# Query copies moved around VectorE's exps in a graph-attention kernel, and the last layers' loads put in program order on one queue

## The chip, the cores and the metric

The kernel runs on one core of one Trainium2 chip. The metric is the device time of one execution in microseconds. The kernel before the change takes 11197.88 us (median of three runs, 11197.59 to 11198.84).

## What is computed

Four graph layers run over the same 3327 x 128 features `x` and the same 3327 x 3327 float32 adjacency `adj`. Each layer adds its result to its input and normalises the rows.

```python
# layer 0: attention; d is the feature (128 of them act as heads), h has 8 values
q = (x @ Wq.T).reshape(d, n, h)          # likewise k and v
a = einsum('dnh,dmh->dnm', q, k) * scale + adj + adj
x = layernorm(x + einsum('dnm,dmh->dnh', softmax(a, axis=2), v).reshape(n, h*d) @ Wo.T)
# layer 1: x = layernorm(x + dinv * (adj + I) * dinv @ (x @ W.T + b)),  dinv = (row sums of adj + I)**-0.5
# layer 2: x = layernorm(x + (adj / row sums) @ x @ W_in + (adj.T / column sums) @ x @ W_out)
# layer 3: x = layernorm(x + x @ W_self.T + (adj @ x) @ W_neigh.T + b)
```

In layer 0 there are 128 score matrices of 3327 x 3327 whose exps have to be formed; that is most of the work.

## The kernel before

**Preparation** (the first 430 us of the trace) forms the projections of q, k and v in DRAM (`q_s`, `k_s`, `v_img`) and starts to write a tiled transpose of the adjacency (`adjT_s`).

**Attention** (`attention()`, about 430 to 10410 us) goes through 28 blocks. A block combines 476 query columns (`CW`) with one of four sets of key tiles, `KBS`, with 7, 7, 6 and 6 tiles of 128 keys: "7-tile" and "6-tile" blocks below. In a block, the 128 features are taken in 32 groups of 4 (`GROUP`). Group number `n` counts on over the blocks (0 to 895); even and odd groups are treated differently.

For each of the 4 features d of a group, three sets of key tiles follow one another (`SETS`: 3 + 2 + 2 tiles, or 2 + 2 + 2). One such set is called a place here; a group has 12. At each place:

- TensorE forms the scores into one of three PSUM tiles `sc` (L572; `kt` and `qt` are its operands). `sc` keeps the adjacency and adds only the difference between this feature and the one before it, which is why `qt` needs negated copies of the features' neighbours.
- ScalarE takes the exp of the tile into `e` (L580). In even groups the third set of the first feature is taken by VectorE instead: `vector_exp` reads the scores once (L536) and then works out the exp with eight more steps (L537, L538, L539, five times L542). In this document these eight are "the chain".
- TensorE weighs the values with the exps of the *group before* into the PSUM tile `o` (L597, `weigh`); at which places it does so is fixed in `PLACES`. The e tiles of VectorE belong to the third set, so that their weighs come late in the odd group that follows.

After every third group `flush` adds `o` to an accumulator on VectorE (L610, or L608 in the first set of keys).

**VectorE's order.** The orders of TensorE, ScalarE, VectorE and GpSimd in this part are those of the program. VectorE's smaller steps wait in a Python list `vec` and are handed out by `vector_work` at each place, as many as a count of estimated times (`clock`) allows; `weigh` forces out what a weigh needs. An entry of `vec` holds its cost, the group it belongs to (`of`; None for copies) and the step.

`copy_queries` gives the three steps that complete the next group's `qt` after its load: L465 and L466 write the negated neighbours into rows 32 to 63, L467 copies rows 0 to 63 into rows 64 to 127. Before, they are put at the *front* of `vec` at the second feature of each group:

```python
elif d % GROUP == 1 and n + 1 < len(groups):
    vec[0:0] = copy_queries(*groups[n + 1])
```

`load_heads` loads `qt` and `kt` two groups ahead from SyncE's queue (L435, L442). Every eighth group VectorE also works on a piece of the adjacency's transpose (`background_work`, L200 to L215).

**The last layers** (about 10410 us to the end) finish layer 0 and do layers 1 to 3. In the first stage, 26 row tiles are loaded from `o_s` (L1051, `divide`), divided (DVE L1053, GpSimd L1055), transposed (L1063), multiplied by `woT` (L1072, `outputs`), added to a tile of `x` (L88) and normalised. Then `gather` runs 26 times for layer 1, and again for layers 2 and 3: each loads 1.7 MB of `adjT_s` (tile `eT`, L1032) and does 26 matmuls (L1038). Layer 2 has also a pass over rows of `adj` (tile `a2`, L1141). `eT` and `a2` share five buffers (`big`). Before, even row tiles are loaded from SyncE's queue and odd ones from ScalarE's; only TensorE's order is fixed (`tc.manual_schedule`), and a scheduler chooses the order of the other engines, SyncE's loads among them.

Of the kernel before, what the change touches and what calls it, by code (L numbers as in the profile page):

```python
# [19 lines left out]
P = 128  # L20
GROUP = 4
# [29 lines left out]
def kernel(ctx: ExitStack, tc: tile.TileContext, x, adj, wq, wk, wv, wo,  # L51
# [14 lines left out]
    nc = tc.nc  # L66
    N, D = x.shape
# [18 lines left out]
    def load_rows(eng, sb, dram, t):  # L86
        for a, n in spans(tokens(t)):
            eng.dma_start(out=sb[a:a + n, :], in_=dram[t * P + a:t * P + a + n, :])  # L88

    def store_rows(eng, dram, sb, t):  # L90
        for a, n in spans(tokens(t)):
            eng.dma_start(out=dram[t * P + a:t * P + a + n, :], in_=sb[a:a + n, :])
# [29 lines left out]
    adjT_s = scratch.tile([T * P, T * P], F32, name="adjT_s")  # L122
# [258 lines left out]
    def attention():  # L381
        with tc.tile_pool(name="acc", bufs=1) as accp, tc.tile_pool(name="kq", bufs=3) as kq, \
# [129 lines left out]
            def prepare(b, d):  # L512

                n = b * NHG + d // GROUP
                if d % GROUP == 0:
                    if n + 2 < len(groups):
                        heads[groups[n + 2]] = load_heads(*groups[n + 2])
                    if n + 1 < len(groups):
                        values[groups[n + 1]] = load_values(*groups[n + 1])
                    while stores:  # L520
                        store(*stores.pop(0))
                    background(n)
                elif d % GROUP == 1 and n + 1 < len(groups):
                    vec[0:0] = copy_queries(*groups[n + 1])
                elif d % GROUP == 3:
                    background_work(n)

            vec = []
# [423 lines left out]

    w1T, w2, w3T, woT = (act.tile([P, w], F32, name=f"tw{i}") for i, w in enumerate((D, 2 * D, 2 * D, HD)))
    for sb, dram in ((w1T, w1T_s), (w3T, w3T_s), (woT, woT_s)):
        nc.sync.dma_start(out=sb, in_=dram)  # L955
    nc.sync.dma_start(out=w2[:, 0:D], in_=w2_in)
    nc.sync.dma_start(out=w2[:, D:2 * D], in_=w2_out)
    b1_sb = act.tile([1, D], F32, name="b1_sb")
    nc.sync.dma_start(out=b1_sb, in_=b1.unsqueeze(0))
    b3_sb = act.tile([1, D], F32, name="b3_sb")  # L960
    nc.sync.dma_start(out=b3_sb, in_=b3.unsqueeze(0))


    for i in range(4):
# [61 lines left out]
    def gather(t, y, col, b, meanwhile=()):  # L1026


        n = tokens(t)
        todo = list(meanwhile)  # L1030
        e = big.tile([P, T, P], F32, tag="big", name="eT")
        (nc.sync, nc.scalar)[t % 2].dma_start(out=e.rearrange("p s n -> p (s n)"), in_=adjT_s[t * P:(t + 1) * P, :])  # L1032
        ps = bank(b)
        for s in range(T):
            while todo and todo[0][0] <= s:
                todo.pop(0)[1]()
            m = tokens(s)
            nc.tensor.matmul(ps[:n, 0:D], lhsT=e[:m, s, :n], rhs=y[:m, s, col:col + D],  # L1038
                             start=(s == 0), stop=(s == T - 1))
        for _, what in todo:  # L1040
            what()
        return ps
# [48 lines left out]
        nc.vector.tensor_tensor(xs[1][:n, t, :], ps[:n, 0:D], xs[0][:n, t, :], ALU.add)  # L1091
        nc.scalar.copy(y3[:n, t, :], ps[:n, D:2 * D])

    with tc.manual_schedule(engines={mybir.EngineType.PE}):
        def stage0(t):
            if t < T:
                heads_turned(t)
            if 1 <= t <= T:
                outputs(t - 1)
            if 3 <= t <= T + 2:  # L1100
                turn(xs[0], t - 3, 4)
            if 4 <= t <= T + 3:
                support(t - 4)

        for t in range(T):
            divide(t)
            stage0(t)


        def after(src, t, finish):  # L1110
            return [(12, lambda: turn(src, t, 4)), (19, lambda: finish(t))] if t >= 0 else []

        for t in range(T):
            n = tokens(t)
            ps = gather(t, y1, 0, 6 + t % 2,
                        after(xs[1], t - 1, messages) if t else
                        [(2 + 5 * k, lambda k=k: stage0(T + k)) for k in range(4)])
            z = work.tile([P, D], F32, name="z")
            nc.vector.tensor_tensor(z[:n, :], ps[:n, 0:D], y1[:n, t, :], ALU.add)
            h = work.tile([P, D], F32, name="h")  # L1120
            nc.vector.scalar_tensor_tensor(h[:n, :], z[:n, :], dinv[:n, t:t + 1], xs[0][:n, t, :],
                                           ALU.mult, ALU.add)
            norm(n, h[:n, :], xs[1][:n, t, :])


        backT = act.tile([P, NP], F32, name="backT")
        cols = [(c, min(512, N - c)) for c in range(0, N, 512)]
        order = [6, 0, 1, 2, 3, 4, 5]
        acc = {}
        for t in range(T):  # L1130
            n = tokens(t)
            a = big.tile([P, T * P], F32, tag="big", name="a2")
            load_rows((nc.sync, nc.scalar)[t % 2], a[:, 0:N], adj, t)
            for i, (c, w) in enumerate(cols):
                if t == 0 and i == 3:
                    turn(xs[1], T - 1, 4)
                if t == 0 and i == 5:
                    messages(T - 1)
                if t == 0:
                    acc[i] = bank(order[i])  # L1140
                nc.tensor.matmul(acc[i][:, 0:w], lhsT=y2[:n, t, D:2 * D], rhs=a[:n, c:c + w],  # L1141
                                 start=(t == 0), stop=(t == T - 1))
        for i, (c, w) in enumerate(cols):
            copy(i, backT[:, c:c + w], acc[i][:, 0:w])


        for t in range(T):
            n = tokens(t)
            zs = {}

            def back(t=t, n=n):
                pb = bank(t % 2)
                nc.tensor.transpose(pb[:n, 0:P], backT[:, t * P:t * P + n], ident)  # L1153
                zs[t] = work.tile([P, D], F32, name="z")
                nc.vector.scalar_tensor_tensor(zs[t][:n, :], pb[:n, 0:D], inv_col[:n, t:t + 1], xs[1][:n, t, :],
                                               ALU.mult, ALU.add)

            ps = gather(t, y2, 0, 7 - t % 2, [(6, back)] + after(xs[0], t - 1, last_inputs))
            h = work.tile([P, D], F32, name="h")
            nc.vector.scalar_tensor_tensor(h[:n, :], ps[:n, 0:D], inv_row[:n, t:t + 1], zs[t][:n, :],  # L1160
                                           ALU.mult, ALU.add)
            norm(n, h[:n, :], xs[0][:n, t, :])


        for t in range(T):
            n = tokens(t)
            ps = gather(t, y3, 0, 6 + t % 2, after(xs[0], T - 1, last_inputs) if t == 0 else ())
            h = work.tile([P, D], F32, name="h")
            nc.vector.tensor_tensor(h[:n, :], ps[:n, 0:D], xs[1][:n, t, :], ALU.add)
            res = work.tile([P, D], F32, name="res")  # L1170
            norm(n, h[:n, :], res[:n, :])
            store_rows(nc.sync, out, res, t)


# [27 lines left out]
```

## Time and profile before

| what | value |
|---|---|
| median of three runs | 11197.88 us |
| profiled execution, its own time | 11193.06 us |
| its span, first to last instruction | 11191.2 us |
| mean granted TensorE clock | 0.988 |
| busy: TensorE, ScalarE, VectorE, GpSimd | 94%, 88%, 65%, 13% of the span |
| attention, first exp to last | 431 to 10407 us |
| a 7-tile block, a 6-tile block | about 372 us, about 340 us |
| last layers | 10410 to 11191 us |

A profile line begins with the source line and the engine: PE is TensorE's matmuls, PEld its weight loads, DVE VectorE, ACT ScalarE, POOL GpSimd, SP SyncE; a q behind an engine's name marks its sequencer, which also issues DMAs. Then come the operation, the tile written and the tiles read, the shape and the count. In the groups of the page, the numbers behind the bar are busy time in us and the mean of one in ns; behind the second bar stand the engine's idle time just before these instructions and what ended most of it. In a list of waits, a line gives the waiting engine and line, what it waited for, and then total us, times and the longest. In a timeline, a line gives the start and length in us; the idle time before it stands in brackets. Windows give busy time and instruction counts of each engine in a stretch, and at the end the granted clock, the DMA engines' share and GB/s. TensorE's ends are modelled, so that its busy time overstates how full it is.

### The profile page before, as it was taken

What the parts mean: (1) busy time and instruction counts of PE and PEld (TensorE: products, weight loads), DVE (VectorE), ACT (ScalarE), POOL (GpSimd) and SP (SyncE); (2) the same over time, 40 slices, a digit from 0 to 9 for tenths busy, and PEclk for the clock granted to TensorE, in tenths of its full rate; (3) what the DMA queues carried; (4) which work ended last, traced back from release to release, by engine and by line L of the source; (5) the groups of instructions that cost most, each with busy time, mean ns of one, the idle gap of its engine ahead of it and who ended that gap; (6) DMA issues with size and microseconds to landing.
All of it is one profiled execution on the core that took longest, in us unless ns stands there. A gap on an engine that the chain in (4) does not pass through costs nothing. (4 is left out here: it accounts for less than half of the span.)

```text
span 11191.2 us, 200920 instructions
## 1 busy us (share of the span) xinstructions
PE 10524.8 (94%) x76607; PEld 4034.8 (36%) x76607; DVE 7265.7 (65%) x8368; ACT 9856.7 (88%) x10746; POOL 1497.4 (13%) x2738
## 2 busy tenths in 40 slices
PE   6699999999999999999999999999999999999899
PEld 2233333333333333333333333333333333333779
DVE  6466777667776677766777666776666666666412
ACT  2599999999999999999999999999999999999400
POOL 4311122111121111211112100010000100000200
PEclk8799999999999999999999999999999999999999
DMA  8888888888888888888888888778887788877686
GB/s 288 197 126 123 124 128 133 123 127 125 127 132 123 127 126 128 130 126 127 124 128 130 122 121 120 119 118 119 116 114 114 115 118 116 115 109 113 192 284 245
DMA packets 989911, 1536.50 MB, mean 137 GB/s; under 512 B 202879, under 2 KB 799921, under 8 KB 974617
## 3 DMA queue, kind: packets, MB, share of 16 engines
q1 hardware_dynamic: 894410, 1292.54, 74.4%
q0 software_dynamic: 82432, 128.80, 4.5%
q10 hardware_dynamic: 12110, 102.22, 2.6%
q8 instruction: 621, 10.17, 0.5%
q14 instruction: 338, 2.77, 0.1%
HBM read 1378.68 MB, written 143.98 MB: 136 GB/s over the span
## 5 line engine op out<-in xcount | busy, mean ns | idle before, releaser
L580 ACT ACTIVATE e<-sc 128x952 f32<-128x952 f32 (+1 forms) x10304 | 9667.4, 1062 | 332.8 <-PE sc L572 294.8
L597 PE MATMUL o<-e,v_pad 128*32 128x476 f32 (+1 forms) x46592 | 5633.3, 573 | 227.6 <-DVE e L542 176.7
L572 PE MATMUL sc<-qt,kt 64*128 64x476 f32 x23296 | 4473.0, 438 | 187.2 <-ACT e L580 136.0
L572 PEld LDWEIGHTS sc<-qt,kt 64*128 64x128 f32 x23296 | 2170.2, 184 | 4510.2 <-ACT e L580 4229.0
L536 DVE TENSOR_SCALAR ey<-sc 128x952 f32<-128x952 f32 x448 | 515.1, 1150 | 2543.1 <-PE sc L572 2543.1
L597 PEld LDWEIGHTS o<-e,v_pad 128*32 128x32 f32 (+1 forms) x46592 | 1037.0, 108 | 2144.4 <-issue 1848.2
L542 DVE SCALAR_TENSOR_TENSOR e<-e,ey 128x952 f32<-128x952 f32 x1344 | 1545.0, 1150 | 38.6
L481 POOL COPY v_pad<-vs 128x192 f32<-128x192 f32 (+1 forms) x896 | 337.5, 403 | 8543.4 <-DMA vs<-v_img 5980.0
L467 DVE CAST qt<-qt 64x1904 fp32r<-64x1904 f32 x896 | 1035.6, 1156 | 30.5
L224 POOL DMA_DIRECT2D adjT_s<-at x1352 | 800.0, 599 | 223.3 <-DMA adjT_s<-at 82.7
L465 DVE TENSOR_SCALAR qt<-qt 32x1428 fp32r<-32x1428 f32 x896 | 803.8, 897 | 36.9 <-DMA qt<-q_s 13.9
L538 DVE SCALAR_TENSOR_TENSOR ey<-et,ey 128x952 f32<-128x952 f32 x448 | 515.9, 1152 | 15.5
L542 DVE SCALAR_TENSOR_TENSOR e<-e,et 128x952 f32<-128x952 f32 x448 | 515.3, 1150 | 10.7
L542 DVE SCALAR_TENSOR_TENSOR e<-ey 128x952 f32<-128x952 f32 x448 | 513.1, 1145 | 0.0
L1038 PE MATMUL bank<-y,eT 128*128 128x128 f32 (+1 forms) x4056 | 473.9, 276 | 0.4 <-DVE h L1160 0.4
L1038 PEld LDWEIGHTS bank<-y,eT 128*128 128x128 f32 (+1 forms) x4056 | 465.3, 192 | 5.7 <-DVE h L1160 0.6
L466 DVE TENSOR_SCALAR qt<-qt 32x476 fp32r<-32x476 f32 x896 | 353.0, 394 | 4.5 <-DMA qt<-lead_s 3.7
L610 DVE TENSOR_TENSOR acc<-o,acc 128x476 f32<-128x476 f32 x231 | 150.2, 650 | 251.7 <-PE o L597 251.1
L539 DVE TENSOR_SCALAR et<-et 128x952 int32<-128x952 int32 x448 | 294.7, 658 | 15.4
L537 DVE TENSOR_SCALAR et<-ey 128x952 f32<-128x952 f32 x448 | 294.9, 658 | 13.9
L1003 ACT ACTIVATE rstd<-mv,eps 128x1 f32<-128x1 f32 x104 | 30.7, 295 | 302.6 <-DVE mv L1001 297.1
L330 ACT ACTIVATE hi<-pp 128x1024 fp32r<-128x1024 f32 x52 | 52.8, 1025 | 177.7 <-PE pp L281 147.5
(148 smaller groups left out, 2407.5 us busy)
## 6 DMA issues: line engine op xcount, KB each, us to landing
kt<-k_s SPq DMA_DIRECT2D x5320, 96.0 KB
kt<-k_s SPq DMA_DIRECT2D x1764, 128.0 KB
qt<-q_s SPq DMA_DIRECT2D x896, 119.0 KB
qt<-q_s SPq DMA_DIRECT2D x1792, 59.5 KB
eT<-adjT_s ACTq DMA_DIRECT2D x39, 1664.0 KB
eT<-adjT_s SPq DMA_DIRECT2D x39, 1664.0 KB
vs<-v_img SPq DMA_DIRECT2D x224, 224.0 KB
adjT_s<-at POOLq DMA_DIRECT2D x1352, 32.0 KB, 4.9
```

The costliest lines, as they stand in the source:

```text
L224: nc.gpsimd.dma_start(out=flat_ap(adjT_s, (t * P + 32 * q) * NP + c * PIECE, [[NP, 32], [P, ns], [1, P]]), in_=at[32 * i:32 * i + 32].rear ...
L465: return [(0.9, None, lambda: nc.vector.tensor_scalar(qt[32:64, 1:], qf[0:32, 0:GROUP - 1], -1.0, None, ALU.mult)), (0.4, None, lambda: nc ...
L466: (0.4, None, lambda: nc.vector.tensor_scalar(qt[32:64, 0], before, -1.0, None, ALU.mult)),
L467: (1.2, None, lambda: nc.vector.tensor_copy(qt[64:128], qf[0:64]))]
L481: nc.gpsimd.tensor_copy(vp[:, 32:32 + nt * GROUP * 32].rearrange("p (x c) -> p x c", c=32)[:, :, 0:H], vs.rearrange("p (x c) -> p x c", c=H))
L536: nc.vector.tensor_scalar(y, x, -58 * math.log(2.0), 2 / math.log(2.0), ALU.max, ALU.mult)
L538: vec.append((1.2, of, lambda: nc.vector.scalar_tensor_tensor(y, t, ROUND, y, ALU.subtract, ALU.subtract)))
L542: vec.append((1.2, of, lambda i=i, a=a: nc.vector.scalar_tensor_tensor(e, e if i else y, a, t if i == len(POLY) - 1 else y, ALU.add, ALU.m ...
L572: nc.tensor.matmul(s[:, i, 0:CW], lhsT=kt[64 * rg:64 * rg + 64, k, pos * P:(pos + 1) * P], rhs=qt[64 * rg:64 * rg + 64, k, :], start=False ...
L580: nc.scalar.activation(e[:, 0:n, :], s[:, 0:n, 0:CW], AF.Exp, scale=2.0)
L597: nc.tensor.matmul(o[32 * j:32 * j + 32, 0:CW], lhsT=values[b, g][:m, c:c + 32], rhs=es[b, g * GROUP + j, r][:m, :], start=(r == 0 and u = ...
L1038: nc.tensor.matmul(ps[:n, 0:D], lhsT=e[:m, s, :n], rhs=y[:m, s, col:col + D], start=(s == 0), stop=(s == T - 1))
```

## The change

In attention, the copies of the next group's queries are appended at the *end* of `vec`: at the first feature of even groups, before that group's L536 and its chain exist, and at the second feature of odd groups, behind what is left of the chain. Before a group's loads are issued, the pending copies of the list are forced out.

In the last layers, SyncE's order is the program's too (it joins TensorE in `manual_schedule`). All loads of `eT` and `a2` come from SyncE. The seven loads of weights and biases move from SyncE's to ScalarE's queue, and the stores of the result from SyncE's to GpSimd's. Three lines are added in front of L536, so that it and all later lines have numbers that are higher by 3 in the changed kernel.

```diff
                 if d % GROUP == 0:
+                    while any(of is None for _, of, _ in vec):
+                        vec.pop(0)[2]()
                     if n + 2 < len(groups):
                         heads[groups[n + 2]] = load_heads(*groups[n + 2])
...
                     background(n)
-                elif d % GROUP == 1 and n + 1 < len(groups):
-                    vec[0:0] = copy_queries(*groups[n + 1])
-                elif d % GROUP == 3:
+
+                if d % GROUP == n % 2 and n + 1 < len(groups):
+                    vec.extend(copy_queries(*groups[n + 1]))
+                if d % GROUP == 3:
                     background_work(n)
...
     for sb, dram in ((w1T, w1T_s), (w3T, w3T_s), (woT, woT_s)):
-        nc.sync.dma_start(out=sb, in_=dram)
-    nc.sync.dma_start(out=w2[:, 0:D], in_=w2_in)
+        nc.scalar.dma_start(out=sb, in_=dram)
+    nc.scalar.dma_start(out=w2[:, 0:D], in_=w2_in)
...
-        (nc.sync, nc.scalar)[t % 2].dma_start(out=e.rearrange("p s n -> p (s n)"), in_=adjT_s[t * P:(t + 1) * P, :])
+        nc.sync.dma_start(out=e.rearrange("p s n -> p (s n)"), in_=adjT_s[t * P:(t + 1) * P, :])
...
-    with tc.manual_schedule(engines={mybir.EngineType.PE}):
+    with tc.manual_schedule(engines={mybir.EngineType.PE, mybir.EngineType.SP}):
...
-            load_rows((nc.sync, nc.scalar)[t % 2], a[:, 0:N], adj, t)
+            load_rows(nc.sync, a[:, 0:N], adj, t)
...
-            store_rows(nc.sync, out, res, t)
+            store_rows(nc.gpsimd, out, res, t)
```

More of the change, by code (lines that the diff above doesn't have):

```diff
@@ L954 @@
     for sb, dram in ((w1T, w1T_s), (w3T, w3T_s), (woT, woT_s)):
-        nc.sync.dma_start(out=sb, in_=dram)
-    nc.sync.dma_start(out=w2[:, 0:D], in_=w2_in)
-    nc.sync.dma_start(out=w2[:, D:2 * D], in_=w2_out)
+        nc.scalar.dma_start(out=sb, in_=dram)
+    nc.scalar.dma_start(out=w2[:, 0:D], in_=w2_in)
+    nc.scalar.dma_start(out=w2[:, D:2 * D], in_=w2_out)
     b1_sb = act.tile([1, D], F32, name="b1_sb")
-    nc.sync.dma_start(out=b1_sb, in_=b1.unsqueeze(0))
+    nc.scalar.dma_start(out=b1_sb, in_=b1.unsqueeze(0))
     b3_sb = act.tile([1, D], F32, name="b3_sb")
-    nc.sync.dma_start(out=b3_sb, in_=b3.unsqueeze(0))
+    nc.scalar.dma_start(out=b3_sb, in_=b3.unsqueeze(0))
     for i in range(4):
```

## The prediction

> **What bounds the kernel now.** I read the page first, then the waits block by block, then the timelines of three engines over one pair of groups. On the page, ScalarE's exps (L580) fill nearly the whole middle, and what ends their idle time is TensorE's scores.
>
> ```profile
> PE 10524.8 (94%) x76607; PEld 4034.8 (36%) x76607; DVE 7265.7 (65%) x8368; ACT 9856.7 (88%) x10746; POOL 1497.4 (13%) x2738
> ...
> L580 ACT ACTIVATE e<-sc 128x952 f32<-128x952 f32 (+1 forms) x10304 | 9667.4, 1062 | 332.8 <-PE sc L572 294.8
> L597 PE MATMUL o<-e,v_pad 128*32 128x476 f32 (+1 forms) x46592 | 5633.3, 573 | 227.6 <-DVE e L542 176.7
> ```
>
> The second row shows the lever: TensorE stands 176.7 us before L597, waiting for e tiles that VectorE makes (L542). The list of waits has it 223 times. The windows of one 6-tile and one 7-tile block (sum columns: PE, PEld, DVE, ACT, POOL busy) say where:
>
> ```profile
> 8644.00:8984.00 340.00, 322.39 (x2335) 106.21 (x2333) 230.75 (x252) 321.75 (x369) 31.82 (x67) 1.00 0.79 119
> 8985.00:9356.00 371.00, 358.93 (x2703) 127.97 (x2695) 230.64 (x252) 368.26 (x368) 17.59 (x41) 1.00 0.82 116
> ```
>
> In the 7-tile block ScalarE idles 2.7 us of 371: it is the bound there. In the 6-tile block both it and TensorE idle 18 us of 340. The waits of that block:
>
> ```profile
> PEld o L597 <- DVE e L542: 19.1, 16, 1.4
> ACT e L580 <- PE sc L572: 17.3, 36, 2.1
> ```
>
> 16 waits, one per odd group; the 7-tile block's list has no such row. 14 blocks of 6 tiles times 16 is 224, against 223 counted: every odd group of a 6-tile block stalls once, and no other. The timelines of VectorE, TensorE and ScalarE over one (start, us):
>
> ```profile
> 5883.97 0.89 DVE L465 TENSOR_SCALAR qt<-qt 32x1428 fp32r<-32x1428 f32 x1
> ...
> 5890.02 3.52 DVE L542 SCALAR_TENSOR_TENSOR e<-e,ey 128x952 f32<-128x952 f32 x3
> 5893.55 0.90 DVE L465 TENSOR_SCALAR qt<-qt 32x1428 fp32r<-32x1428 f32 x1
> ...
> 5895.95 1.15 DVE L542 SCALAR_TENSOR_TENSOR e<-e,et 128x952 f32<-128x952 f32 x1
> 5899.80 0.65 DVE L610 TENSOR_TENSOR acc<-o,acc 128x476 f32<-128x476 f32 x1 [2.70 <-PE o L597]
> 5903.62 1.15 DVE L536 TENSOR_SCALAR ey<-sc 128x952 f32<-128x952 f32 x1 [3.17 <-PE sc L572]
> ```
> ```profile
> 5897.16 1.01 PE L597 MATMUL o<-e,v_pad 128*32 128x476 f32 x8 [0.74 <-DVE e L542]
> ```
> ```profile
> 5882.50 15.62 ACT L580 ACTIVATE e<-sc 128x952 f32<-128x952 f32 x18 [0.33 <-PE sc L572]
> 5898.62 4.39 ACT L580 ACTIVATE e<-sc 128x952 f32<-128x952 f32 x5 [0.49 <-PE sc L572]
> ```
>
> The second set of copies (5893.55) stands in front of the last chain step, which ends at 5897.10; TensorE starts at 5897.16 after 0.74 us; its next scores are late and ScalarE breaks off 0.49 us. The break of 0.33 us at 5882.50 is another: two weighs in a row at the start of every even group, and it has nothing to do with VectorE.
>
> **What the Trainium skill says.** "Perfetto Trace Analysis", Tensor Engine Instruction (MATMUL, LD_WEIGHTS): ScalarE, VectorE and GpSimd are strict FIFO. The trace agrees: the last step waited behind copies that nobody needed yet. So the order of VectorE's queue alone decides. "DMA: Bandwidth & Descriptors", Issuing engines are not separate DMA queues: loads from any engine share the same 16 engines and interleave. The trace agrees (below: loads of o are slow while adjacency loads run). The same page, Specifications: a first byte takes about 1 us from GpSimd, 0.6 us from SyncE. "TensorE: Matmul & The Clock Gate", What's actually happening: the clock halves after an idle window of about 3.4 us. The trace has granted 0.66 in 10480:10490, among idle gaps of 2.15 and 2.52 us.
>
> **Part 1, the copies.** No instruction is added or removed; 896 sets of three (L465, L466, L467: 0.897 + 0.394 + 1.156 = 2.45 us busy, 2.40 from start to start of what follows) change places. Before, two sets stand between L536 and the chain's last step. After, as the built queue shows, one is ahead of L536 and the other behind the last step. The chain then ends 2 x 2.40 = 4.8 us earlier, at 5892.3. TensorE asked at 5897.16 - 0.74 = 5896.42, so 4.1 us are left, and the wait goes in all 224 groups. A flush (0.65 us) inside the chain or the transposes' work (always behind it) fits in that.
>
> *Worth:* within a run ScalarE starts an exp every 0.85 us ((4.39 - 0.96) / 4 = 0.86). The exp before the break began at 5882.50 + 15.62 - 0.97 = 5897.15, the next at 5898.62: 1.47, so 0.62 lost; the deepest break seen beside it (0.69 idle, at 5835.66) gives 0.8. I take 0.65: 224 x 0.65 = **146 us**. Low end: the idle of about 0.50 alone, 112. High end: all of TensorE's wait, 177. TensorE can follow: its 17.6 us of idle in the block hold 12 or so of this wait, and 5 remain. The 7-tile blocks gain nothing.
>
> *What may be late instead.* (a) L536 in an even group with copies ahead of it. Worst is behind a flush: L610 starts 5899.80 on TensorE's release, ends 5900.45, the copies run to 5902.9, and L536's scores come at 5903.62: 0.7 us spare. In an odd group made 0.65 us shorter the flush moves along, so the spare stays. Without a flush the spare is over 3 us. Cost 0; low end -0, high end 0.3 us in some 70 groups, 20. (b) Even groups' copies, now behind the chain, end near 5894.7; their group's first scores come some 5 us later. Cost 0. (c) Odd groups' copies come 3 places (2.5 us) earlier than before; their loads were issued a group ago, and L465 waited only 13.9 us for DMA in all 896 sets. Cost 0, either way 10. (d) SyncE's loads of heads that wait for L466 (42.5 us of its waits) see it earlier or within the same group: 0.
>
> **Part 2, the last layers** (10410 to the end). From 10545 on TensorE is 100% busy in every window, so queue changes there give nothing; what can move is the first stage and the end.
>
> ```profile
> 10457.67 0.33 SPq L1032 DMA_DIRECT2D eT<-adjT_s  x1
> ...
> 10463.31 7.65 SPq L1051 DMA_DIRECT2D o<-o_s  x3
> ```
> ```profile
> 10463.24 0.33 PE L1013 MATMUL bank<-ident,x 128*128 128x128 f32 x1 [2.27 <-ACT xT L1015]
> ...
> 10476.48 0.30 PE L1013 MATMUL bank<-ident,x 128*128 128x128 f32 x1 [2.15 <-DVE x L1005]
> ...
> 10482.76 0.47 PE L1013 MATMUL bank<-ident,x 128*128 128x128 f32 x1 [2.52 <-ACT xT L1015]
> ```
>
> Each gap follows a pair of 1.7 MB adjacency loads put among the loads of o and x.
> 1. Seven weight loads leave SyncE: the first o load is issued at 10416.1, not 10419.85. About -3 us (high end 0, if woT's 512 KB compete as much on ScalarE's queue).
> 2. Adjacency loads behind all 26 loads of o: the three gaps and one of 1.06 go, -8, and with them the half clock, 10 x 0.34 = -3.4. High end 0.
> 3. Later prefetch: the first adjacency load is issued when tile 22 of 26 is through, three or four stages of 3.55 us ahead of its use; TensorE eats a tile in 6.35 us, and 1.70 MB at the 304 GB/s of window 10700:10800 is 5.6 us. 0; high end +31 (five loads of prefetch lost).
> 4. SyncE alone instead of SyncE and ScalarE: an issue takes 0.33 us every 6.35. 0.
> 5. Stores of the result from GpSimd: only the last two count. Two issues at 0.6 instead of 0.81 together, 0.4 more, and a longer landing (5.6 us median for o_s stores, under load): +2, ends +0.5 and +5.
>
> Sum -3 - 11.4 + 2 = **-12 us**.
>
> **Sum.** 146 + 12 = 158. The profiled execution took 11193.06 us (span 11191.2): 11035. The median is 4.8 above it, so 11197.88 - 158 = **11040 us**.
>
> **Rivals.**
> - *TensorE takes over.* In the even groups of 6-tile blocks it is never idle for long; if its weighs, not ScalarE, set the pace once the wait is gone, half comes back: -73 - 12, 11113. For it: the 0.33 us break stays. Against: 5 us of idle left per block. 0.10.
> - *The last layers lose.* Point 3 at its high end: -146 + 31 - 1, 11082. 0.07.
> - *L536 late.* If the copies ahead of it wait for their loads, VectorE stands with the scores bank occupied. In a plain even group over 3 us are free first; the bank's next scores give some 0.6 more. To be slower than before, all 448 even groups must lose more than 158/448 = 0.35 us each, so L536 must come 4 us late; at 0.7 us lost it is +314 - 158, 11354. Against: 13.9 us of DMA waits before L465 in all. 0.03.
> - *The order doesn't change on the chip:* FIFO and the built queue leave 0.01, 11198.
>
> **How the numbers follow.** 0.79 for the forecast, whose own ends are 112 + 0 and 177 + 18: 11086 and 11003. Trimmed to eight in ten with the rivals below slower: 11018 to 11082. A measurement of this kernel tells 0.2%, 22 us, from no change. Of the 0.96 of the first three cases 0.01 may end within it, and the last rival does: faster 0.95, same 0.02, slower 0.03.
>
> **What would show it.** The row L597 <- DVE e is gone or under 20 us; a 6-tile block takes about 330 us instead of 340, a 7-tile block still 371; ScalarE's runs in 6-tile blocks break once a pair instead of twice; L536 still waits for sc L572. In the first stage of the last layers no gap over 1 us after 10430. Wrong if L572 begins to wait for ey L536 or for qt, or if L1038 waits for DMA eT.

## The result and the profile after

The changed kernel takes **11061.93 us** (median of four runs, 11057.42 to 11066.37), the kernel before 11197.74 us beside it (four runs, 11193.82 to 11198.84). The ratio is 0.9879, with a 95% interval from 0.9862 to 0.9896: 135.8 us less. The forecast was 158 less, 11040, with a range of 11018 to 11082.

The profiled execution of the changed kernel took 11066.37 us itself (span 11064.6), 4.4 us above its median. The page first, with the rows that answer to those shown of before; their lines are numbered 3 higher:

```profile
PE 10517.7 (95%) x76607; PEld 4050.4 (37%) x76607; DVE 7309.3 (66%) x8368; ACT 9830.9 (89%) x10746; POOL 1588.4 (14%) x2765
...
L583 ACT ACTIVATE e<-sc 128x952 f32<-128x952 f32 (+1 forms) x10304 | 9643.7, 1067 | 215.4 <-PE sc L575 182.6
L600 PE MATMUL o<-e,v_pad 128*32 128x476 f32 (+1 forms) x46592 | 5637.7, 573 | 40.0 <-DVE acc L613 37.1
...
L465 DVE TENSOR_SCALAR qt<-qt 32x1428 fp32r<-32x1428 f32 x896 | 800.6, 893 | 417.6 <-DMA qt<-q_s 331.9
```

The counts are the same as before but for GpSimd's 27 stores of the result. L600 no longer waits for an e of VectorE: 176.7 us of such waits are gone, and what is left is the flush. ScalarE's idle time before its exps falls from 332.8 to 215.4 us. The last row is the new thing: VectorE's first copy waits 331.9 us for its query loads, where it waited 13.9 before:

```profile
L465 DVE TENSOR_SCALAR qt<-qt 32x1428 fp32r<-32x1428 f32 x896 | 803.8, 897 | 36.9 <-DMA qt<-q_s 13.9
```

Most of that is idle time of an engine with time to spare; some of it is not, as will be seen.

The windows of the same 6-tile block and the same 7-tile block, with the same columns as before:

```profile
8542.00:8871.60 329.60, 321.61 (x2339) 107.35 (x2341) 231.16 (x252) 319.91 (x370) 38.31 (x67) 1.00 0.84 122
8872.00:9244.00 372.00, 359.61 (x2708) 128.19 (x2696) 231.13 (x252) 368.72 (x368) 20.75 (x42) 1.00 0.84 117
```

The 6-tile block takes 330 us instead of 340 with the same work in it; the 7-tile block is as long as it was. The waits of the 6-tile block have no row for an e of VectorE any more, and ScalarE's wait in it falls from 17.3 to 9.3 us:

```profile
ACT e L583 <- PE sc L575: 9.3, 23, 2.1
...
DVE qt L465 <- DMA qt<-q_s: 7.0, 5, 3.9
```

VectorE's timeline over one pair of groups, and ScalarE's beside it:

```profile
5823.97 1.15 DVE L539 TENSOR_SCALAR ey<-sc 128x952 f32<-128x952 f32 x1 [5.09 <-PE sc L575]
...
5828.78 3.52 DVE L545 SCALAR_TENSOR_TENSOR e<-e,ey 128x952 f32<-128x952 f32 x3
5832.34 1.15 DVE L545 SCALAR_TENSOR_TENSOR e<-e,et 128x952 f32<-128x952 f32 x1
5833.52 0.89 DVE L465 TENSOR_SCALAR qt<-qt 32x1428 fp32r<-32x1428 f32 x1
```
```profile
5823.68 19.88 ACT L583 ACTIVATE e<-sc 128x952 f32<-128x952 f32 x23 [0.36 <-PE sc L575]
5843.89 2.77 ACT L583 ACTIVATE e<-sc 128x952 f32<-128x952 f32 x3 [0.32 <-PE sc L575]
```

The chain runs through without copies in it and ends 9.5 us after L539's start (5833.49); the copies stand behind. ScalarE makes all 23 exps of the pair in one run: the break in the odd group is gone, that at the start of each even group stays.

**Where the 126.6 us between the two spans (11191.2 and 11064.6) went.** I cut both traces at the first exp, at the first exp of the last group, and at TensorE's last weigh; the durations of groups are the distances of their first exps.

| stretch | before | after | difference |
|---|---|---|---|
| preparation, to the first exp | 431.3 | 439.4 | +8.1 |
| attention: odd groups, 6-tile blocks | 2492.3 | 2336.2 | -156.1 |
| even groups, 6-tile blocks | 2256.5 | 2261.6 | +5.1 |
| odd groups, 7-tile blocks | 2664.2 | 2657.4 | -6.9 |
| even groups, 7-tile blocks | 2551.6 | 2568.4 | +16.8 |
| last weigh to the end | 781.1 | 787.5 | +6.4 |

(The last group, 14.2 us in both, is the rest.) Two things are wrong in the forecast's terms: about 17 us of loss in even groups of 7-tile blocks, where none was expected, and a loss of 6.4 us in the last layers, where a gain of 12 was. The 8.1 us of preparation are the same instructions in both; over the twelve profiles of this study the first exp came at 429.5 to 442.6 us, with the lowest from a kernel that has the attention's change, so this term is spread between runs and no effect.

### The profile page after: what moved, and what is told of

The parts are those of the page before. It is cut to its first block, busy times and chain, and to the rows that moved or that the text cites. A ratio compares the mean times of both kernels' runs of the same rounds, so it can differ in the third digit from the quotient of the medians.

```text
span 11064.6 us, 201055 instructions
## 1 busy us (share of the span) xinstructions
PE 10517.7 (95%) x76607; PEld 4050.4 (37%) x76607; DVE 7309.3 (66%) x8368; ACT 9830.9 (89%) x10746; POOL 1588.4 (14%) x2765
## 5 line engine op out<-in xcount | busy, mean ns | idle before, releaser
L583 ACT ACTIVATE e<-sc 128x952 f32<-128x952 f32 (+1 forms) x10304 | 9643.7, 1067 | 215.4 <-PE sc L575 182.6
L600 PE MATMUL o<-e,v_pad 128*32 128x476 f32 (+1 forms) x46592 | 5637.7, 573 | 40.0 <-DVE acc L613 37.1
L575 PE MATMUL sc<-qt,kt 64*128 64x476 f32 x23296 | 4474.6, 438 | 240.6 <-ACT e L583 167.0
L575 PEld LDWEIGHTS sc<-qt,kt 64*128 64x128 f32 x23296 | 2186.2, 184 | 4552.6 <-ACT e L583 4258.1
L600 PEld LDWEIGHTS o<-e,v_pad 128*32 128x32 f32 (+1 forms) x46592 | 1037.5, 108 | 1942.6 <-issue 1901.8
L539 DVE TENSOR_SCALAR ey<-sc 128x952 f32<-128x952 f32 x448 | 515.1, 1150 | 1670.0 <-PE sc L575 1669.6
L481 POOL COPY v_pad<-vs 128x192 f32<-128x192 f32 (+1 forms) x896 | 427.9, 503 | 8286.2 <-DMA vs<-v_img 6658.8
L465 DVE TENSOR_SCALAR qt<-qt 32x1428 fp32r<-32x1428 f32 x896 | 800.6, 893 | 417.6 <-DMA qt<-q_s 331.9
L541 DVE SCALAR_TENSOR_TENSOR ey<-et,ey 128x952 f32<-128x952 f32 x448 | 516.0, 1152 | 15.5
L1041 PE MATMUL bank<-y,eT 128*128 128x128 f32 (+1 forms) x4056 | 473.9, 276 | 0.8 <-DVE h L1163 0.4
L1041 PEld LDWEIGHTS bank<-y,eT 128*128 128x128 f32 (+1 forms) x4056 | 465.3, 192 | 6.1 <-DVE h L1163 0.6
L466 DVE TENSOR_SCALAR qt<-qt 32x476 fp32r<-32x476 f32 x896 | 356.1, 397 | 4.8 <-DMA qt<-lead_s 3.7
L1006 ACT ACTIVATE rstd<-mv,eps 128x1 f32<-128x1 f32 x104 | 30.6, 294 | 316.3 <-DVE mv L1004 316.3
```

The lines of the kernel that those rows point to most:

```text
L465: return [(0.9, None, lambda: nc.vector.tensor_scalar(qt[32:64, 1:], qf[0:32, 0:GROUP - 1], -1.0, None, ALU.mult)), (0.4, None, lambda: nc ...
L466: (0.4, None, lambda: nc.vector.tensor_scalar(qt[32:64, 0], before, -1.0, None, ALU.mult)),
L481: nc.gpsimd.tensor_copy(vp[:, 32:32 + nt * GROUP * 32].rearrange("p (x c) -> p x c", c=32)[:, :, 0:H], vs.rearrange("p (x c) -> p x c", c=H))
L539: nc.vector.tensor_scalar(y, x, -58 * math.log(2.0), 2 / math.log(2.0), ALU.max, ALU.mult)
L541: vec.append((1.2, of, lambda: nc.vector.scalar_tensor_tensor(y, t, ROUND, y, ALU.subtract, ALU.subtract)))
L575: nc.tensor.matmul(s[:, i, 0:CW], lhsT=kt[64 * rg:64 * rg + 64, k, pos * P:(pos + 1) * P], rhs=qt[64 * rg:64 * rg + 64, k, :], start=False ...
```

## The experiments

All ratios are to the kernel before, run on the same chip. "Attention" below is from the first exp to the first exp of the last group: 9964.6 us before, 9823.6 after. Six of the kernels, the changed one among them, have exactly the same order of VectorE in this part; their profiles show 9821.4 to 9834.5 us for it, so a difference of some 10 us in the attention of two single profiles means nothing by itself. The odd groups repeat much better: 2335.3 to 2336.2 us in 6-tile blocks, 2657.1 to 2658.7 in 7-tile blocks.

**1. Each half alone.** `attn_only` is the kernel before with the edit of `prepare` alone, `tail_only` the kernel before with the rest alone.

```diff
+                    while any(of is None for _, of, _ in vec):
+                        vec.pop(0)[2]()
...
-                elif d % GROUP == 1 and n + 1 < len(groups):
-                    vec[0:0] = copy_queries(*groups[n + 1])
+                if d % GROUP == n % 2 and n + 1 < len(groups):
+                    vec.extend(copy_queries(*groups[n + 1]))
```

> The kernel before with the attention's edit alone; the last layers as before. Theory (the whole gain is the wait of TensorE for VectorE's chain in the odd groups of 6-tile blocks, and the last layers lose): attention 9964.6 to about 9824 us, so 11197.7 - 141 = 11057 us, a few us below the changed kernel, with the span from the last first-form exp to the end as in the kernel before. Rival (the last layers do bring what was forecast for them, 12 us, and attention less): about 11074. Rival (the 8.1 us by which the preparation was longer in the profile of the changed kernel belong to the attention's edit): the first exp again at about 439 us and the sum about 11065.

> The kernel before with the edits of the last layers alone. Theory: stores from GpSimd's queue add about 5 us at the end, the start of the first stage about 2, the first stage keeps its length within 1 us, the gathers stay at 651.1: 11197.7 + 6 = 11204 us. Forecast on record: 12 us faster, 11186. Rival (SyncE in the program's order has no effect that can be measured): 11198.

Measured: `attn_only` 11055.68 us, ratio 0.9872 [0.9857, 0.9887]; attention 9834.5, its last layers 778.7. `tail_only` 11202.04 us, ratio 1.0003 [0.9995, 1.0012]; attention 9963.1, its last layers 786.0. The whole gain is the attention's; the rest brings none of its forecast 12 us and costs 4.9 us by the windows against the kernel before (786.0 and 781.1) and 7.4 against `attn_only`; the old last layers took 778.7 to 781.6 us in three profiles, the new ones 786.0 to 787.5 in six. In the total of `tail_only` that is 3.8 us, inside its interval; the windows are what shows it. The preparation of `attn_only` is the shortest of all (429.5), so its edit does not lengthen it.

**2. Which of the two moves counts, and what the other costs.** `half` leaves the even groups' copies where they stood (in front of the chain's rest) and has only the odd groups' behind the chain; `ahead_only` was meant to do the reverse. The edits to the changed kernel, `half` first:

```diff
-                if d % GROUP == n % 2 and n + 1 < len(groups):
-                    vec.extend(copy_queries(*groups[n + 1]))
+                if d % GROUP == 1 and n + 1 < len(groups):
+                    if n % 2:
+                        vec.extend(copy_queries(*groups[n + 1]))
+                    else:
+                        vec[0:0] = copy_queries(*groups[n + 1])
```
```diff
-                    vec.extend(copy_queries(*groups[n + 1]))
+                    vec[0:0] = copy_queries(*groups[n + 1])
```

> The changed kernel, but in even groups the copies stand where they stood before (in front of what is left of the chain, from the second place on, behind the first operation of the exp); in odd groups behind the chain, as changed. Theory (VectorE's chain needs to be earlier by less than one group of copies, and the 17 us that the attention loses elsewhere come from L539 standing behind copies that wait for their query loads): the chain ends about 2.4 us later than in the changed kernel and 2.4 us earlier than before, L600 still waits for no e of VectorE, L539 no longer comes late in the third group of a column's start, attention about 9808 us, total about 11046 us. Rival (the spare between chain and TensorE is smaller than 2.4 us): L600 waits for DVE e again, 0.3 us in each of 224 odd groups, about 11130. Rival (the 17 us have another cause than the place ahead of L539): no change, 11062.

> The changed kernel, but in odd groups the copies stand in front of what is left of the chain, as before; in even groups ahead of the first operation of the exp, as changed. Theory: the chain again ends 2.4 us earlier than before, which is enough, so L600 waits for no e; L539 comes late in the third group of a column's start as in the changed kernel, so 11062 us, the same within 0.1%. Rival (it is the odd groups' place behind the chain that brings the gain): close to the kernel before, 11190 or more. Rival (the loss of 17 us comes from the odd groups' place): 11046.

Measured: `half` 11059.48 us, ratio 0.9877 [0.9862, 0.9892], attention 9820.0. `ahead_only` 11062.18 us, ratio 0.9879 [0.9864, 0.9895], attention 9826.9. The odd groups of the 6-tile blocks come to 2342.0 and 2335.5 us (2492.3 before).

`ahead_only` is no test of half the move: **it is the changed kernel itself, instruction for instruction.** With the even groups' copies ahead of the chain, the chain has left `vec` before the odd groups' copies enter it, so that nothing is left for them to stand behind, and front and end of the list are the same place; in both traces the chain of 6-tile blocks is 9.5 us long. The even groups' move alone therefore brings the whole 4.8 us, and the new place in odd groups adds nothing to it. `half` is a test: its chain is 12.0 us long (14.3 before), and its odd 6-tile groups still gain 150.3 of the 156.1 us. **2.4 us take nearly the whole wait away,** and the other 2.4 meet hardly any.

The even groups of 7-tile blocks show what "ahead of L539" costs: 2551.5 us in `half`, which is the figure of before (2551.6), against 2565.2 to 2575.0 in the six profiles of the changed attention. So the loss is in that place. But `half` is not 15 us faster as expected: its odd groups give back 7.8 us (7-tile) and 5.8 us (6-tile) against the changed kernel. In the 7-tile blocks that is only the figure of before again (2665.1; 2664.2 before). The rival of a smaller spare was far off (11130); a small part of it may be there; what takes the 5.8 us was not followed further.

**3. Where L539 comes late.** Group by group, 15.5 of the 16.8 us lie in one: the third group of a block that begins a new column of queries (5.2 us in group 2, 4.8 in group 258, 3.6 in 386, 1.6 in 130). VectorE's timeline of the changed kernel in group 2, then ScalarE's:

```profile
471.95 0.89 DVE L465 TENSOR_SCALAR qt<-qt 32x1428 fp32r<-32x1428 f32 x1 [15.59 <-DMA qt<-q_s]
472.77 0.39 DVE L466 TENSOR_SCALAR qt<-qt 32x476 fp32r<-32x476 f32 x1
473.19 1.15 DVE L467 CAST qt<-qt 64x1904 fp32r<-64x1904 f32 x1
474.37 1.15 DVE L539 TENSOR_SCALAR ey<-sc 128x952 f32<-128x952 f32 x1
```
```profile
465.07 7.42 ACT L583 ACTIVATE e<-sc 128x1428 f32<-128x1428 f32 x7
476.38 3.07 ACT L583 ACTIVATE e<-sc 128x952 f32<-128x952 f32 x3 [3.89 <-PE sc L575]
```

The copies for group 3 stand ahead of L539 and wait for loads that have not landed. L539 starts with them out of the way at 474.37, its scores hold their PSUM tile until then, and ScalarE has nothing to do for 3.89 us. `early` puts the copies in their old place in the third group of every block (`n % NHG == 2`), the first block of a column or not.

```diff
-                if d % GROUP == n % 2 and n + 1 < len(groups):
-                    vec.extend(copy_queries(*groups[n + 1]))
+                late = n % NHG == 2
+                if d % GROUP == (1 if late else n % 2) and n + 1 < len(groups):
+                    at = 0 if late else len(vec)
+                    vec[at:at] = copy_queries(*groups[n + 1])
```

> The changed kernel, but in the third group of each block (the one whose copies wait for their query loads in the trace) the copies stand where they stood before: one place later, in front of what is left of the chain. Theory (the even 7-tile groups lose 17 us only there, because L539 stands behind copies whose loads have not landed; the rest of the edit costs nothing and gains everything): even 7-tile groups back from 2568.4 to about 2551.6 us, odd groups as in the changed kernel (2657.4 and 2336.2), attention 9823.6 - 17 = 9807 us, total about 11045 us. Rival (the loads are late in any case and TensorE then waits for them elsewhere, as in the kernel with all even groups moved back, where the odd groups took back 13.6 us): attention 9815 us or more, 11053 or more.

Measured: 11050.51 us, ratio 0.9868 [0.9851, 0.9884]; attention 9813.8, between the two expectations (9807 and 9815). Even 7-tile groups are back at 2551.9 us, 16.5 less, so the cause is shown. But the odd ones take back 7.2 (2664.5), 6.3 of them in the *fourth* group of the same blocks. Both are then the figures of before (2551.6 and 2664.2): the exception returns the 7-tile blocks to where they were, and all that is won lies in the 6-tile blocks. What is late next is not the query but the values. The waits of `early` around group 131, where the fourth group lost most:

```profile
POOL v_pad L481 <- DMA vs<-v_img: 43.0, 2, 29.6
...
PEld o L602 <- POOL v_pad L481: 2.5, 1, 2.5
PE o L602 <- POOL v_pad L481: 2.1, 1, 2.1
```

TensorE's weigh waits for GpSimd's copy of the values, and GpSimd for their load. These waits suggest that at the start of a column several loads are late together, and that the order on VectorE has a say in which of them is felt; no run isolates it.

**4. The start and the end of the last layers.** From the last weigh to the first transpose of the first stage (L1066) the changed kernel takes 20.4 us, 18.2 before. The first load of o is early as forecast, but GpSimd does not take it up. SyncE's, VectorE's and GpSimd's timelines of the changed kernel there:

```profile
10283.09 1.40 SPq L1054 DMA_DIRECT2D o<-o_s  x2
```
```profile
10287.58 0.95 DVE L1056 RECIPROCAL rec<-o 128x128 f32<-128x128 f32 x1 [0.96 <-DMA o<-o_s]
10291.68 0.95 DVE L1056 RECIPROCAL rec<-o 128x128 f32<-128x128 f32 x1 [3.14 <-DMA o<-o_s]
10293.99 0.95 DVE L1056 RECIPROCAL rec<-o 128x128 f32<-128x128 f32 x1 [1.18 <-DMA o<-o_s]
```
```profile
10295.10 6.96 POOL L1058 TENSOR_TENSOR on<-o,rec 128x1024 f32<-128x1024 f32 x3 [14.65 <-DVE rec L1056]
```

The first reciprocal ends at 10288.53, the first division starts at 10295.10, after the third one. The trace names the third reciprocal as what released it, but that can hardly be so: the division needs only the first, and in `ahead_only`, the same program, it starts at 10291.93, when the third ends at 10292.07. And at the other end, the store of the last rows, first SyncE's in the kernel before, then GpSimd's in the changed one:

```profile
11176.11 12.38 SPq L92 DMA_DIRECT2D out_dram<-res  x4
```
```profile
11056.43 1.10 POOL L92 DMA_DIRECT2D out_dram<-res  x2 [5.22 <-DVE res L1008]
```

Before, the last issue ends at 11188.49 and the span at 11191.2, 2.7 us later. After, the last issue ends at 11057.53 and the span at 11064.6, 7.1 us later. That is not a later landing: by the semaphore that tells of it, the last store has landed 1.1 us after the end of its issue in the changed kernel, and 1.0 us after it in the kernel before. What ends late is GpSimd itself, whose last instructions are DRAINs. The kernel before first, then the changed one; behind the count stand the shortest, the median and the longest in ns, and the starts of the first and the last:

```profile
L1197 POOLq DRAIN  x3: 46/113/6408, 10521.7 to 11191.0; - x3
```
```profile
L1200 POOLq DRAIN  x3: 50/113/6863, 11056.9 to 11064.3; - x3
L1200 SPq DRAIN  x3: 7/7/13, 11059.2 to 11064.0; - x3
```

The long one is the first of the three. In the kernel before, GpSimd has it behind it at 10528, 4.0 us after the end of its last division; in the changed kernel it begins with the last stores and lasts until 11063.7, while SyncE, which waits for the stores to land, is done at 11059.3. The other engines then wait for GpSimd alone. `tail_mend` puts the seven weight loads back on SyncE and the stores on ScalarE:

```diff
-        nc.scalar.dma_start(out=sb, in_=dram)
+        nc.sync.dma_start(out=sb, in_=dram)
...
-            store_rows(nc.gpsimd, out, res, t)
+            store_rows(nc.scalar, out, res, t)
```

> The changed kernel with the weights back on SyncE's queue and the results stored from ScalarE's. Theory for the end (a store from GpSimd lands later): from the last matmul to the end 10.2 to about 5.4 us. Theory for the start (the weights on ScalarE's queue delay GpSimd's first division, though the o load itself comes earlier): first turn 18.2 us after the last weigh instead of 20.4. Together 11062 - 7 = 11055 us. Rivals: if the end stays near 10, it is SyncE's or the stores' order and not the queue; if the first turn stays at 20.4, it is not the weights' queue but the order of SyncE's loads (written out by hand) that delays it, and the total is 11057.

Measured: 11056.18 us, ratio 0.9876 [0.986, 0.9893]. Its last layers take 779.6 us instead of 787.5; the first transpose comes 18.1 us after the last weigh, and from the first matmul of the gathers to the end of the span it takes 656.0 us, 661.4 after and 656.5 before. VectorE's and GpSimd's timelines at the start, and ScalarE's at the end:

```profile
10284.88 0.95 DVE L1056 RECIPROCAL rec<-o 128x128 f32<-128x128 f32 x1 [4.15 <-DMA o<-o_s]
```
```profile
10286.47 6.97 POOL L1058 TENSOR_TENSOR on<-o,rec 128x1024 f32<-128x1024 f32 x3 [12.40 <-DMA o<-o_s]
```
```profile
11047.24 1.06 ACTq L92 DMA_DIRECT2D out_dram<-res  x2
```

The first division now follows the first reciprocal by 0.64 us, and the span (11050.3) ends 2.0 us after the last issue; GpSimd's long DRAIN is over at the end of the first stage again. Both causes are shown: weights on ScalarE's queue at the start, stores on GpSimd's at the end, though not by the later landing that was expected of them. *Why* weights on ScalarE hold GpSimd's first division for 6 us is not shown: GpSimd had nothing else to do.

**5. The first stage, where 11 us were to be had.** The gaps of 2 us behind adjacency loads are gone, as forecast, and the half clock at 10480 with them, yet the stage (first transpose to first gather) takes 105.8 us, 106.4 before; over the kernels with GpSimd's division, old queue order and new, it takes 103.8 to 106.4. The prediction had counted on the 3.55 us a tile of the stretches without a gap; after, one tile follows the other (by the starts of L1078) every 4.2 to 4.8 us in the middle of the stage. In the waits of the changed kernel between 10300 and 10400 us TensorE stands 0.6 us in 17 tiles:

```profile
PE bank L1066 <- ACT oT L1067: 9.7, 17, 0.6
```

My first theory was ScalarE's order, which puts rstd (L1006), and with it a wait for VectorE, ahead of both copies of oT. `act_order` fixes ScalarE's order as the program's:

```diff
-    with tc.manual_schedule(engines={mybir.EngineType.PE, mybir.EngineType.SP}):
+    with tc.manual_schedule(engines={mybir.EngineType.PE, mybir.EngineType.SP, mybir.EngineType.Activation}):
```

> The changed kernel with ScalarE too in the program's order in the last layers: the two oT copies of a tile then stand ahead of the previous tile's rstd. Theory (the forecast 11 us of the first stage were taken back because both oT copies stand behind an rstd that waits for DVE mv, 0.6 us of TensorE in nearly every tile): L1066 no longer waits 0.6 us for ACT oT, the first stage goes from 105.8 to about 94 us (24 tiles by about 0.5), total about 11051 us. Rival (another member of the cycle takes over, VectorE's 2.5 us operation L1008 or GpSimd's division): the wait is named otherwise and the stage stays at 103 to 106 us, 11062.

Measured: 11067.2 us, ratio 0.9881 [0.9865, 0.9898]; the stage takes 105.4. That theory fell: the wait went to another name, in the waits of the same stretch,

```profile
PE bank L1016 <- ACT xT L1018: 7.1, 17, 0.8
...
PE bank L1066 <- ACT oT L1067: 0.6, 1, 0.6
```

and nothing was won. What it left as the cause was an engine that is full. The groups of the first stage by line, first of the kernel before (the lines there are L1055 and L1005), then of the changed one; behind the bar stand busy us and mean ns:

```profile
L1055 POOL TENSOR_TENSOR on<-o,rec 128x1024 f32<-128x1024 f32 x25 | 58.6, 2356 | 48.5 <-PE bank L1063 16.4 <-DVE rec L1053 14.2 <-DMA o<-o_s 12.5
L1005 DVE TENSOR_SCALAR x<-h,mv,rstd 128x128 f32<-128x128 f32 x21 | 17.7, 843 | 0.7
```
```profile
L1058 POOL TENSOR_TENSOR on<-o,rec 128x1024 f32<-128x1024 f32 x25 | 58.8, 2353 | 54.8 <-DVE rstd L1007 30.7 <-DVE rec L1056 21.5 <-PE bank L1066 2.5
L1008 DVE TENSOR_SCALAR x<-h,mv,rstd 128x128 f32<-128x128 f32 x23 | 49.8, 2166 | 0.9
```

GpSimd's division takes 2.35 us in both. VectorE's small scaling of 128 columns takes 0.84 us on average before and 2.17 after; tile by tile it is 0.35 alone and up to 2.52; 2.4 us or more in 2 of 26 tiles before, in 18 after. In those 18 it starts 0.07 us ahead of a division and ends 0.08 us after it; where it starts 1.12 us after the division's start it takes 1.3 us, and again ends 0.08 us after it. So it lasts until the division is over. With 2.51 us for it, VectorE's six operations of a tile come to 0.28 + 0.29 + 0.18 + 0.95 + 0.10 + 2.51 = 4.31 us, about the new pitch, and VectorE is busy for 60.83 of 65 us in the middle of the stage:

```profile
10330.00:10395.00 65.00, 54.96 (x433) 49.42 (x431) 60.83 (x88) 24.12 (x73) 35.33 (x15) 1.00 0.54 150
```

`div_vector` takes GpSimd out of it (on top of `tail_mend`):

```diff
-        nc.gpsimd.tensor_tensor(ons[t][:n], o[:n, 0:H, :], rec[:n, :].unsqueeze(1).to_broadcast([n, H, D]), ALU.mult)
+        nc.vector.tensor_tensor(ons[t][:n], o[:n, 0:H, :], rec[:n, :].unsqueeze(1).to_broadcast([n, H, D]), ALU.mult)
```

> The kernel with the weights back on SyncE and the stores on ScalarE, and the division of L1058 on VectorE instead of GpSimd. Theory (in the first of the last stages VectorE is the bound: its L1008 takes 2.51 us instead of 0.35 wherever it starts with GpSimd's division, and the eight operations of a tile then fill 4.3 us): with GpSimd silent L1008 takes 0.35 us every time, the division costs VectorE about 1.2 us (the 952 columns of L545 take 1.15), so 3.4 us of VectorE a tile instead of 4.3, and TensorE sets a pitch of 3.45 to 3.6 us as in the undisturbed tiles of the kernel before; the stage goes from 105.4 to about 92 us, the total from 11056 to about 11043. Rival (the pitch of 4.1 to 4.5 us is set elsewhere: by the landing of the o loads, or by the half clock of TensorE): L1008 short, but the stage at 102 us or more.

Measured: 11048.74 us, ratio 0.9867 [0.985, 0.9883]; the stage takes 92.7 us, 105.4 in `tail_mend`. The groups of its first stage, and a window of it:

```profile
L1058 DVE TENSOR_TENSOR on<-o,rec 128x1024 f32<-128x1024 f32 x24 | 29.3, 1222 | 0.5
...
L1008 DVE TENSOR_SCALAR x<-h,mv,rstd 128x128 f32<-128x128 f32 x23 | 7.8, 340 | 0.4
```
```profile
10300.00:10380.00 80.00, 78.43 (x638) 73.06 (x638) 66.68 (x150) 37.31 (x104) 0.00 (x0) 0.99 0.63 175
```

VectorE does the division in 1.22 us and the scaling in 0.34 each time; although it has taken on GpSimd's work, it has less to do, and TensorE is now busy for 78.43 of 80 us. The division itself became shorter in the same step (1.22 us instead of 2.35), so the run doesn't separate that from the end of the hold-up. The 11 us that the forecast looked for are there, behind a bound that it did not see.

**6. What is worth keeping.** `best_attn` is the kernel before with the attention's edit and `early`'s exception, and the last layers as before. `best_both` has the same attention and the last layers of `div_vector`.

> The kernel before with the attention's edit, the third group of each block as before, and the last layers as before: the two halves of the change that the runs showed to be worth keeping. By the windows: attention 9814 us instead of 9964.6, last layers unchanged, 11197.7 - 151 = 11047 us; 11042 if the waits in the fourth group stay small as in the kernel with all even groups moved back, 11055 if the repair is worth nothing.

> The changed kernel with the third group of each block as before, the weights on SyncE, the stores on ScalarE and the division on VectorE. If the three repairs add up: attention 9814, first turn 18.2, first stage about 92, end 5.4 us: 11062 - 10 - 7 - 13 = 11032 us. If the division brings nothing: 11045.

Measured: `best_attn` 11046.28 us, ratio 0.9863 [0.9846, 0.9879], attention 9812.6. `best_both` **11034.83 us** (11031.91 to 11039.52), ratio 0.9854 [0.9837, 0.987], attention 9813.5, first stage 93.2, last layers 766.6 us. It was expected at 11032: the repairs add up, and its median lies 27 us below the changed kernel's.

## Why the prediction was right, and where it was not

- **Part 1, the wait of 224 odd groups: right.** 146 us were forecast, 156 measured in those groups: 0.67 us in an ordinary one (10.99 to 10.32) and 0.75 where a flush falls into it, against 0.65 taken. The 6-tile block came to 330 us, ScalarE's runs break once a pair, and no e of VectorE is waited for. The reckoning of 4.8 us holds too (the chain's length went from 14.3 to 9.5 us); `half` shows that 2.4 of it were nearly enough. That attention as a whole came to 141 is in part luck: 10 us more than forecast in these groups and 7 in the odd ones of 7-tile blocks stand against 22 lost in even groups.
- **(a), (b), (d): right within a few us.** SyncE's waits for L466 fell from 42.5 to 6.9 us. L539 still waits for its scores and is not held up behind a flush; the even groups of 6-tile blocks lost 5 us in all.
- **(c), cost 0, either way 10: mis-sized.** It cost 17 us in the even groups of 7-tile blocks (14 to 23 in the six profiles of this attention). "Their loads were issued a group ago, and L465 waited only 13.9 us" was read at the copies' old place, where VectorE came later; a wait that is short there says nothing of a place 2.5 us earlier, and the list of waits after shows 331.9 us. Nearly all of them fall on idle time of VectorE, as the step assumed; those at the start of a column have L539 behind them. In the even groups, moreover, it is the first operation that they stand ahead of, and (a) looked only at a flush there. This is the mechanism of the rival "L536 late", in one group of some blocks instead of in all 448. The sign of being wrong that the prediction named for it came in small: L575 waits for ey L539 41.4 us in 35 waits, where L572 waited 14.9 us in 20.
- **Part 2, item 1, weights off SyncE, -3: wrong in sign.** The o load and the first reciprocal did come earlier; GpSimd's division did not follow, +2.2.
- **Item 2, adjacency loads behind the loads of o, -11.4: the failed step.** The gaps went, and the stage stayed within 1 us. The working took TensorE's pitch of the undisturbed tiles for the bound everywhere and had no term for VectorE. Before, the scaling already took 0.25 to 2.5 us from tile to tile, a sign that was there to be read; with the disturbance gone the scaling and the division fell into step in 18 of 26 tiles. VectorE's 60.83 busy us of 65 show the bound, `div_vector` that the 11 us were real.
- **Items 3 and 4, later prefetch and one queue, 0: right.** First matmul of the gathers to the last matmul: 651.1 us in both.
- **Item 5, GpSimd's stores, +2 with ends +0.5 and +5: at its upper end,** +4.9, **by another mechanism.** The longer landing did not come (1.1 us after the last issue, 1.0 before). The item had no term for GpSimd's DRAIN of 6.86 us, which now stands at the end of the program; that its upper end covers this is luck.

By the windows the terms come to -141.1 for attention (-146 forecast) and +6.4 for the last layers (-12 forecast), together -134.7; the medians differ by 135.8. Of the 22 us between forecast and result, 18 are Part 2's. The 18 us that its range gave Part 2 at best follow from no item: 3 + 11.4 - 0.5 is 13.9.

The rival "TensorE takes over" did not come about: its idle time per odd group fell from 0.92 to 0.34 us, and there still is some. "The last layers lose" was right in sign alone: the mechanism it named, late prefetch, played no part; L1041 waits for eT 0.8 us in all.

## What to carry to other kernels

When work is moved earlier on an engine, its waits for loads have to be judged at the new place, and what is queued behind it decides the price; here 2.4 us of the move were nearly enough and the rest bought a late exp. Before two variants are compared, look whether their instruction orders differ at all: front and end of an empty list are one place. Removing a visible gap pays only up to the next engine's full load, so add up every engine's busy time per tile before pricing the gap, with the durations of the *disturbed* tiles too. An operation whose duration jumps between two values (0.35 and 2.51 us here) may itself be waiting for something that the list of waits doesn't show. And when work moves to another engine's queue at the end of a program, look at what that engine still does after its last work.

## What the runs showed of the hardware

- A VectorE operation of 128 columns that starts together with GpSimd's division of 1024 columns takes 2.51 us instead of 0.35. The Trainium skill, "SBUF — State Buffer", section "SBUF: two separate sides", says that VectorE and GpSimd share a port pair that one of them locks for its whole instruction while the other is blocked; of VectorE's operations it names those in a two-port mode or with two inputs from SBUF. The durations agree with that: whether the operation begins with a division (2.51 us) or 1.12 us later (1.3 us), it ends 0.08 us after it, and with GpSimd silent it takes 0.34. The section gives the pair to whoever starts first; by the records an operation that starts 0.07 us ahead of the division is still held, and one that starts 0.16 us ahead (once, in the kernel before) is not. Not every operation is held, in line with the page: the reciprocal L1056 keeps its 0.95 us in both kernels.
- GpSimd's first DRAIN after its last work ends 6.2 us after the last issue where that work is the result's stores, and 4.0 us after the end of the last division where it is that (6.86 and 6.41 us long); SyncE's DRAINs at the end take 0.14 us at most. With the stores on GpSimd's queue the span ends 7.1 us after the last issue, with those on SyncE's 2.7 us and on ScalarE's 2.0 to 2.3 us. The landing of the last store differs little: 1.1, 1.0 and 0.7 us after its issue.
- The division of 1024 columns takes 2.35 us on GpSimd and 1.22 us on VectorE.
